# The first transfers of a graph-attention kernel: four of them issued from ScalarE's queue, and one warm-up matmul fewer

## The chip, the cores and the metric

The kernel runs on one core of one Trainium2 chip. A core has TensorE (PE; its weight loads are listed as PEld), VectorE (DVE), ScalarE (ACT), GpSimd (POOL) and SyncE (SP), which here only issues transfers. Sixteen DMA engines move the data. The metric is the device time of one execution in microseconds (us); lower is better.

## The reference

A batch of 16 graphs with 512 nodes of 512 features goes through one layer of graph attention with two directions, 16 heads and, as keys and values, only the first 20 nodes of each graph:

```python
q_exp = jnp.where(row_zero[..., None], 0.0, q[:, None, :])
vcq = jnp.concatenate([exp_v, q_exp], axis=-1)
self_feat = vcq @ W_self.T + b_self
output = self_feat
for d in range(2):
    A = adj_f if d == 0 else jnp.swapaxes(adj_f, 1, 2)
    A = A[:, :, :NONGT, :]
    cond = A.sum(-1)
    vb = A @ w_bias + b_bias
    output = output + _gat_attention(self_feat, cond, vb, Wq[d], bq[d], Wk[d], bk[d], Wout[d], bout[d])
rel = jax.nn.relu(output)
return exp_v + rel
```

In `_gat_attention`, `kv = self_feat[:, :20]`, queries and keys are projections of `self_feat` and `kv`, the weights are a softmax over the 20 keys, masked where `cond` is 0, and the weighted values go through `Wout`. Everything is float32.

## The kernel before, in words

The kernel has a setup and a main loop. The setup (lines 345 to 628) works on the 16 × 20 = 320 key rows of all graphs together. It makes their `self_feat` (called kvn and, with the bias, kvT), the projected keys khT, and from khT and Wq the folded keys g, so that the main loop can take scores straight from `self_feat`. The main loop (lines 641 to 721) goes over the 16 graphs, four node tiles of 128 each: `self_feat` of the tile (line 189), scores (line 249), mask and softmax on VectorE, ScalarE and GpSimd, and, one graph behind, the weighted values (line 314) and the store.

The order is written out by hand (`manual_schedule`): the instructions of each engine run in the order of the code. A transfer belongs to the queue of the engine whose name stands before `dma_start`; `nc.sync` is SP's queue. Eight semaphores serve the transfers issued by SP and ScalarE in turn, so that a transfer waits until the eighth before it has landed.

The change lies in the first 20 us of the setup:

- Line 382: warm-up matmuls of a tile of ones, 128 × 128, into `ps_warm`. A float32 matmul appears in the profile as two rows.
- Lines 385 to 390: `rows` issues one transfer from SP. `kv_rows(k, n)` issues rows k × 128 and on of the key rows' transposed input (`xkv`, 160 KB for one k) and of the feature half of W_self (`ws_v`, 256 KB).
- Lines 392 to 414: the transfers in order. `q_sb` is the condition vector (32 KB), `ws_q` the condition half of W_self (1 MB), `bs_sb` the bias b_self (2 KB), `wk_sb` the key weights (2 × 1 MB), `bk_sb` the key bias (4 KB), `wq_sb` the query weights (2 × 1 MB).
- Lines 417 to 419: GpSimd sums the four chunks of `xkv` into `rsk`, from which PE (line 440) makes the row sums that tell zero rows.
- Lines 428 to 454: PE's order is terms 0 and 1 of the key rows (line 423: four matmuls per term, one for each 128 features of the output), the four matmuls with `ws_q` (line 433), term 2, the row sums (line 440), four small matmuls that turn q (line 445), and term 3. ScalarE copies the product of line 433 out (line 437), its first work; the table load of its activation functions stands before it.
- Lines 455 to 465: per 128 features, a product on GpSimd (the first on VectorE), an addition on VectorE (kvn) and the bias `bs_sb` on ScalarE (kvT).
- Lines 468 to 478: `key_rows`, the projection with `wk_sb` (line 472) and the bias `bk_sb` on ScalarE (line 476). The folded keys (line 550) follow with `wq_sb`.

Of the kernel before, what the change touches and what calls it, by code (L numbers as in the profile page):

```python
# [13 lines left out]
P = 128  # L14
# [4 lines left out]
def gat_kernel(  # L19
# [20 lines left out]
    nc = tc.nc  # L40
# [25 lines left out]
    ws_v = const.tile([P, C, F], F32, name="ws_v")  # L66
# [278 lines left out]
    with tc.tile_pool(name="setup", bufs=1) as sp:  # L345
# [6 lines left out]
        bs_sb = sp.tile([P, C], F32, name="bs_sb")  # L352
        bk_sb = sp.tile([P, 2, C], F32, name="bk_sb")
# [10 lines left out]
        with tc.tile_pool(name="setup_k", bufs=1) as sk:  # L364
            xkv = sk.tile([P, C, BM], F32, name="xkv")
# [13 lines left out]
                    base=-k * DH, channel_multiplier=1,  # L379
                )  # L380
            warm = ps_acc.tile([P, 512], F32, tag="acc", name="ps_warm")
            for _ in range(8):
                nc.tensor.matmul(warm[:, :P], ones, ones, start=True, stop=True)

            def rows(sb, src):
                nc.sync.dma_start(sb, src.rearrange("(c p) f -> p c f", p=P))

            def kv_rows(k, n):
                rows(xkv[:, k : k + n], xkvT[k * P : (k + n) * P])
                rows(ws_v[:, k : k + n], wsT[k * P : (k + n) * P])  # L390

            kv_rows(0, 1)
            kv_rows(1, 1)
            nc.sync.dma_start(q_sb, qT)
            rows(ws_q, wsT[F:])
            kv_rows(2, 1)
            kv_rows(3, 1)
            nc.sync.dma_start(bs_sb, b_self)
            for d in range(2):
                rows(wk_sb[d], wkT[d])  # L400
            nc.sync.dma_start(bk_sb, bk)
            for d in range(2):
                rows(wq_sb[:, d], wq[d])
            nc.sync.dma_start(br_sb, b_row.partition_broadcast(P))
# [92 lines left out]
        with tc.tile_pool(name="setup_g", bufs=4) as sg:  # L497
# [102 lines left out]
            for n, runs in enumerate(bursts):  # L600
# [9 lines left out]
                while done * (len(bursts) - first) < (n + 1 - first) * len(other):  # L610
                    f, args = other[done]
# [23 lines left out]
    with tc.manual_schedule():  # L635
# [102 lines left out]
        for ts, ns, width, banks in parts:  # L738
            for q in range(4):
                c = bass.ds(q // 2 * 2, 2)  # L740
# [65 lines left out]
```

## Time and profile before

| | before |
|---|---|
| median of three runs | 634.22 us (633.94, 636.79, 634.22) |
| the profiled execution | 634.41 us |
| its span | 632.6 us |
| PE busy | 618.7 us, 98% of the span |
| VectorE, GpSimd, ScalarE busy | 508.4, 337.4, 218.1 us |
| moved by DMA | 131.86 MB |
| stretch from 0 to 90 us (setup) | DMA engines nearly full |
| stretch from 90 to 607 us (main loop) | PE busy in all of it |

Times inside the profile count from the start of the span. A group's row gives the line, the engine, the operation, the tile written and the tiles read, the shape, and the number of instructions. PE is busy from the start of a matmul to its modelled end, and matmuls overlap, so the distance between two starts, not the length of one, is the pace. In a timeline row the first number is the start, the second the duration of the merged piece, and the bracket has the idle time before it and what ended it. A row of a stretch has for each engine the busy time and, in brackets, the instructions; then the granted clock, the DMA engines' share and GB/s.

### The profile page before, as it was taken

How to read it: one execution, taken by the hardware profiler on the slowest of the kernel's cores; microseconds unless marked ns; L12 is line 12 of the kernel's file. 1: busy time of each engine (PE TensorE's matmuls, PEld its weight loads, DVE VectorE, ACT ScalarE, POOL GpSimd, SP SyncE). 2: the span in 40 equal slices, each digit the busy share in tenths (PEclk: the TensorE clock that was granted, in tenths of full speed). 3: DMA queues.
4: the chain of work that ended last, by engine and by line, in shares of the span. 5: the costliest groups of instructions: out<-in, count | busy, mean ns of one | idle time of the engine just before them, and what ended most of it. 6: DMA issues, size and time to landing. Idle time of an engine off the chain costs nothing.

```text
span 632.6 us, 16385 instructions
## 1 busy us (share of the span) xinstructions
PE 618.7 (98%) x6814; PEld 383.6 (61%) x6814; DVE 508.4 (80%) x815; ACT 218.1 (34%) x480; POOL 337.4 (53%) x258
## 2 busy tenths in 40 slices
PE   8999999999999999999999999999999999999993
PEld 6655459986565656565655656565656565656542
DVE  0566546879888888888888889797988888888886
ACT  1445321233342424242424233343334242424232
POOL 2405331446556464738392938474655646473853
PEclk9999999999999999999999999999999999999997
DMA  8999998628384565738392909292838465663322
GB/s 287 397 382 321 392 371 249 216 88 268 134 237 165 150 253 127 275 90 313 70 333 42 358 19 339 52 292 107 262 141 248 154 207 196 147 256 102 129 68 101
DMA packets 89569, 131.86 MB, mean 208 GB/s; under 512 B 8888, under 2 KB 59608, under 8 KB 87448
## 3 DMA queue, kind: packets, MB, share of 16 engines
q1 hardware_dynamic: 88824, 129.47, 61.7%
q0 software_dynamic: 672, 1.36, 0.8%
q8 instruction: 53, 0.87, 0.6%
q14 instruction: 20, 0.16, 0.1%
HBM read 90.89 MB, written 39.92 MB: 207 GB/s over the span
## 4 chain that ended last, share of the span: by engine, by line
PE 85%; DVE 2%; ACT 1%; issue 0%; DVEq 0%; ACTq 0%
PE ps_s L249 43%; PE ps_sf L189 33%; PE ps_o L314 6%; PE ps_v L523 1%; ACT o L749 0%; PE ps_nz L172 0%; DVE s L287 0%; DVE mx L278 0%; DVE o L745 0%; DVE s L279 0%; PE ps_g(3, 3, 0, 0, 2)0_778 L550 0%; PE ps_g(3, 2, 0, 1, 2)0_752 L550 0%; PE ps_g(3, 1, 1, 0, 2)0_724 L550 0%; PE ps_g(3, 0, 1, 1, 2)0_701 L550 0%; DVE ps_s L276 0%
## 5 line engine op out<-in xcount | busy, mean ns | idle before, releaser
L249 PE MATMUL ps_s<-g,sf 128*64 128x320 f32 x2048 | 287.6, 433 | 0.0
L249 PEld LDWEIGHTS ps_s<-g,sf 128*64 128x64 f32 x2048 | 155.4, 137 | 116.3 <-issue 6.2
L189 PE MATMUL ps_sf<-x,ws_v 128*64 128x256 f32 (+1 forms) x2048 | 222.0, 371 | 0.0
L189 PEld LDWEIGHTS ps_sf<-x,ws_v 128*64 128x64 f32 x2048 | 151.1, 137 | 67.5 <-issue 1.7
L296 POOL TENSOR_TENSOR s<-s,sm 128x640 f32<-128x640 f32 x63 | 80.1, 1271 | 145.5 <-DVE sm L295 134.8
L269 ACT ACTIVATE s<-s 128x640 f32<-128x640 f32 x63 | 46.5, 738 | 220.9 <-DVE s L264 220.9
L239 POOL TENSOR_TENSOR full<-cq,both 128x640 f32<-128x640 f32 x64 | 99.0, 1547 | 27.6 <-ACT both L230 23.5
L211 POOL TENSOR_TENSOR prod<-prod,wb_sb 128x880 f32<-128x880 f32 x32 | 61.3, 1915 | 56.5 <-ACT prod L210 56.5
L260 DVE TENSOR_TENSOR ps_s<-ps_s,full 128x640 f32<-128x640 f32 x63 | 52.3, 831 | 39.4 <-PE ps_s L249 39.4
L336 POOL TENSOR_TENSOR o<-o,x 128x512 f32<-128x512 f32 x60 | 75.5, 1281 | 0.0
L230 ACT COPY both<-add 64x80 f32<-64x80 f32 x128 | 32.8, 256 | 77.4 <-DVE add L225 76.3
L202 DVE SCALAR_TENSOR_TENSOR sf<-nz,qw,ps_sf 128x236 f32<-128x236 f32 (+1 forms) x128 | 52.6, 458 | 3.5 <-PE ps_sf L189 3.5
L333 ACT ACTIVATE o<-o,bo 128x512 f32<-128x512 f32 x60 | 40.0, 714 | 44.3 <-DVE o L327 44.3
L294 DVE TENSOR_REDUCE sm<-s 128x32 f32<-128x640 f32 x63 | 51.6, 818 | 4.4 <-ACT s L269 0.9
L262 DVE TENSOR_REDUCE mx<-ps_s 128x32 f32<-128x640 f32 x63 | 52.0, 825 | 2.2
L264 DVE TENSOR_TENSOR s<-ps_s,mx 128x640 f32<-128x640 f32 x63 | 51.9, 824 | 2.2
L303 DVE STREAM_TRANSPOSE wt<-s 128x640 f32<-128x640 f32 x63 | 52.5, 834 | 0.0
L314 PE MATMUL ps_o<-wt,vd 32*32 32x256 f32 (+2 forms) x2176 | 46.7, 381 | 4.2 <-issue 2.8
L314 PEld LDWEIGHTS ps_o<-wt,vd 32*32 32x32 f32 x2176 | 31.6, 104 | 19.8 <-issue 12.4
L327 DVE TENSOR_TENSOR o<-ps_o,sf 128x512 f32<-128x512 f32 x60 | 36.3, 668 | 0.0
L152 ACT ACTIVATE xn<-xn 128x512 f32<-128x512 f32 x56 | 34.3, 613 | 0.0
L216 DVE TENSOR_REDUCE cond<-adj 128x80 f32<-128x880 int32 x32 | 33.2, 1036 | 0.2 <-DMA adj<-in_adj 0.2
(205 smaller groups left out, 415.7 us busy)
## 6 DMA issues: line engine op xcount, KB each, us to landing
g<-g_d SPq DMA_DIRECT2D x15, 1280.0 KB, 9.0
g_d<-st SPq DMA_DIRECT2D x16, 1120.0 KB, 6.3
x<-in_xT SPq DMA_DIRECT2D x16, 1024.0 KB, 11.0
out_T<-o SPq DMA_DIRECT2D x61, 256.0 KB, 5.0
xn<-in_xn SPq DMA_DIRECT2D x28, 512.0 KB, 8.7
adj<-in_adj SPq DMA_DIRECT2D x32, 440.0 KB, 7.3
vd<-bd_d SPq DMA_DIRECT2D x64, 128.0 KB, 4.1
nz<-nz_d SPq DMA_DIRECT2D x14, 256.0 KB, 4.7
```

The source lines that it names most:

```text
L189: nc.tensor.matmul(held[0][bass.ts(a, R), i * N // 2 : i * N // 2 + hi - lo], ws_v[:, k, bass.ds((2 * f + i) * P + a * R, R)], xs[b][:, k, ...
L202: nc.vector.scalar_tensor_tensor(sfs[b][:, 2 * f + i, lo:hi], nzs[b][:, lo:hi], qw[:, 2 * f + i, b : b + 1], ps[:, i * N // 2 : i * N // 2 ...
L211: nc.gpsimd.tensor_mul(p, p, wb_sb.unsqueeze(1).to_broadcast([P, 2 * S, L]))
L239: nc.gpsimd.tensor_add(f, cqs[b].unsqueeze(1).to_broadcast(shape), adds[b, nt // 2][:, nt % 2].unsqueeze(2).to_broadcast(shape),)
L249: nc.tensor.matmul(ps[bass.ts(a, R), g, : W // 2], sfs[b][:, k, bass.ds(nt * P + g * R, R)], keys[:, k, a], start=(k == 0), stop=(k == C - 1),
L260: nc.vector.tensor_add(pw, pw, fulls.pop((b, nt)).rearrange("p g h m -> p g (h m)"))
L262: nc.vector.tensor_reduce(mx, p4, AX.X, ALU.max)
L264: nc.vector.tensor_sub(s, p4, mx.unsqueeze(3).to_broadcast(full))
L296: nc.gpsimd.tensor_mul(s, s, sm.unsqueeze(3).to_broadcast(full))
L303: nc.vector.transpose(wts[b][:, nt], s.rearrange("p a h m -> p (a h m)"))
L314: nc.tensor.matmul(banks[q][bass.ts(e, DH)].rearrange("p (t n) -> p t n", n=32), vds[b][r, e, i, q // 2 * 2 + n], wt[r, :, bass.ts(j, 32)] ...
L336: nc.gpsimd.tensor_add(o[:, c], o[:, c], xs[b][:, c])
```

## The change

`rows` takes the queue as an argument, and `kv_rows` takes one chunk k and a queue for its weights. The weights of terms 0 and 1 are issued from ScalarE's queue, and behind them, on the same queue, the biases `bs_sb` and `bk_sb`, which stood on SP's queue after term 3 and after the key weights. SP's queue keeps the `xkv` chunks and all the rest in the old order. The warm-up has seven matmuls instead of eight. Nothing else differs, and what is computed is the same.

```diff
@@ -379,26 +379,27 @@
             warm = ps_acc.tile([P, 512], F32, tag="acc", name="ps_warm")
-            for _ in range(8):
+            for _ in range(7):
                 nc.tensor.matmul(warm[:, :P], ones, ones, start=True, stop=True)
 
-            def rows(sb, src):
-                nc.sync.dma_start(sb, src.rearrange("(c p) f -> p c f", p=P))
-
-            def kv_rows(k, n):
-                rows(xkv[:, k : k + n], xkvT[k * P : (k + n) * P])
-                rows(ws_v[:, k : k + n], wsT[k * P : (k + n) * P])
-
-            kv_rows(0, 1)
-            kv_rows(1, 1)
+            def rows(sb, src, queue=nc.sync):
+                queue.dma_start(sb, src.rearrange("(c p) f -> p c f", p=P))
+
+            def kv_rows(k, queue=nc.sync):
+                rows(xkv[:, k : k + 1], xkvT[bass.ts(k, P)])
+                rows(ws_v[:, k : k + 1], wsT[bass.ts(k, P)], queue)
+
+
+            kv_rows(0, nc.scalar)
+            kv_rows(1, nc.scalar)
+            nc.scalar.dma_start(bs_sb, b_self)
+            nc.scalar.dma_start(bk_sb, bk)
             nc.sync.dma_start(q_sb, qT)
             rows(ws_q, wsT[F:])
-            kv_rows(2, 1)
-            kv_rows(3, 1)
-            nc.sync.dma_start(bs_sb, b_self)
+            kv_rows(2)
+            kv_rows(3)
             for d in range(2):
                 rows(wk_sb[d], wkT[d])
-            nc.sync.dma_start(bk_sb, bk)
             for d in range(2):
                 rows(wq_sb[:, d], wq[d])
```

## The prediction

> **What bounds the kernel now.** I read the busy times and the slices of the page first, then the chain of waits, then the busy times of each engine stretch by stretch, and last the instructions of the first 20 us in order of time, because the change touches nothing later.
>
> ```profile
> span 632.6 us, 16385 instructions
> PE 618.7 (98%) x6814; PEld 383.6 (61%) x6814; DVE 508.4 (80%) x815; ACT 218.1 (34%) x480; POOL 337.4 (53%) x258
> PE 85%; DVE 2%; ACT 1%; issue 0%; DVEq 0%; ACTq 0%
> 10.30:12.00 1.70, 1.08 (x9) 0.16 (x8) 0.00 (x0) 0.00 (x0) 0.62 (x1) 1.00 1.01 307
> 19.70:40.00 20.30, 20.17 (x120) 12.77 (x120) 11.53 (x24) 7.82 (x15) 4.46 (x3) 1.00 1.06 406
> 90.00:607.00 517.00, 517.00 (x5904) 325.19 (x5904) 442.64 (x688) 176.11 (x399) 297.11 (x209) 1.00 0.59 188
> ```
>
> The chain is TensorE, and from 19.7 to 607 us PE is idle for about 0.7 us in all (0.13 from 19.7 to 40, 0.56 from 40 to 90, nothing after). So whatever the start gains or loses goes through to the end one for one, and nothing after 20 us can add to it. The only PE idle time that transfers make is in the stretch from 10.3 to 12.0 us (1.70 − 1.08 = 0.62). Here are the rows around it (start, duration, what, and in brackets the idle time before it and its releaser):
>
> ```profile
> 1.06 3.78 PE L383 MATMUL ps_warm<-ones 128*128 128x128 f32 x16 [1.06 <-DVE ones L369]
> 4.63 5.69 PE L423 MATMUL ps_kv<-xkv,ws_v 128*128 128x320 f32 x16
> 10.95 1.05 PE L433 MATMUL ps_q<-ws_q,q_sb 128*16 128x512 f32 x8 [0.62 <-DMA ws_q<-in_wsT]
> 12.01 1.91 PEld L423 LDWEIGHTS ps_kv<-xkv,ws_v 128*128 128x128 f32 x8 [0.93 <-DMA xkv<-in_xkvT]
> 17.81 0.30 PEld L472 LDWEIGHTS ps_k<-kvT,wk 128*128 128x128 f32 x2 [0.30 <-ACT kvT L465]
> ```
>
> PE warms up, does terms 0 and 1 of the key rows (ps_kv), waits for ws_q, then runs nearly without a break. The semaphore records of the trace give the landing of the last of 16 parts: xkv 0 at 3.06, ws_v 0 at 3.86, xkv 1 at 5.01, ws_v 1 at 6.37, q_sb at 6.54, ws_q at 10.81, xkv 2 at 11.24, ws_v 2 at 11.91, xkv 3 at 12.34, ws_v 3 at 13.02, bs_sb at 13.20, wk 0 at 15.76, wk 1 at 18.41, bk_sb at 18.59. Two of these end a wait of PE: ws_q (row at 10.95) and the pair of term 2 (row at 12.01). The issues, and the DMA engines in half-microseconds from 0 to 20 us:
>
> ```profile
> 1.19 0.42 SPq L386 DMA_DIRECT2D ws_v<-in_wsT  x1
> 2.60 0.43 SPq L394 DMA_DIRECT2D q_sb<-in_qT  x1
> 3.08 0.43 SPq L386 DMA_DIRECT2D ws_q<-in_wsT  x1
> DMA  0003989996779999999999999999999999999999
> GB/s 0 0 0 56 311 247 350 290 232 160 156 221 320 315 319 332 369 383 399 405 355 260 281 375 377 406 393 340 377 397 406 378 356 374 410 391 410 406 410 414
> ```
>
> One issue follows another after about 0.475 us (2.60 to 3.08). The engines are nearly full from 2.0 us on, with a dip from 4.5 to 6.0 us.
>
> **Warm-up.** One matmul fewer is two rows of the sixteen: 3.78 us hold 16 starts of 0.213 us, so the first ps_kv matmul may start 2 × 0.213 = 0.43 us earlier, at 4.20, if ws_v 0 is there (it landed at 3.86; its issue now comes 0.45 us earlier). The first starts of L423 lie 0.533 us apart (5.17, 5.70, 6.24, 6.77 in the rows of PE's weight loads), and from 7.2 us on 0.269: the clock comes up near 7.1 us. If it does so at the same moment, 0.43 us are 0.8 of a slow start, so one fast start fewer is left after it: 0.8 × 0.269 = 0.21 us at the end of terms 0 and 1. By itself that is worth nothing, because PE then waits for ws_q (0.62 + 0.21). Its cover is ws_q; if ws_q came early it would be worth its 0.21.
>
> The rows show the step in start distance once, near 7.1 us. [...]
>
> **The stream.** SP now issues xkv 0, xkv 1, q_sb, ws_q: ws_q is fourth and not sixth, so it goes out 2 × 0.475 = 0.95 us earlier (2.13). ScalarE issues ws_v 0 at about 0.74, ws_v 1, bs_sb and bk_sb. The bytes ahead of the end of ws_q are the same, plus two tiny transfers. Their price is in the landings: bs_sb came 0.18 us after ws_v 3, bk_sb 0.18 us after wk 1, both directly behind them in the queue, so 0.36 us for both. Best end: all the earlier issue counts, −0.95 + 0.36 = −0.59; without the tiny ones' price −0.95. Worst end: the engines were full anyway and the start gains nothing, +0.36. Between: the start of the stream. ws_v 0's issue moves from 1.19 to 0.74, and in the slices from 1.5 to 2.5 us only xkv 0 was there to be moved; that is worth up to 0.45, so −0.45 + 0.36 = −0.09. The dip of 4.5 to 6.0 us (156 to 221 GB/s against 290 to 350 before it) says that the bytes alone aren't the limit there, so I take the middle of −0.59 and −0.09, −0.35 us for ws_q. Term 2's pair stands behind ws_q on the same queue and comes with it: also −0.35.
>
> [...]
>
> **What the edit moves past, at no cost.** Eight semaphores serve the transfers in turn, and each new transfer waits for the landing of the eighth before it. In the built order of the changed kernel xkv 2 waits for ws_v 0, ws_v 2 for xkv 0, xkv 3 for xkv 1, ws_v 3 for ws_v 1 (landings 3.06 to 6.37; before: issues at 3.55, 4.10, 4.58, 5.27). They are queued behind ws_q's 1 MB, over 2.5 us of stream at 400 GB/s, so an issue 0.5 us later stays hidden. wk 1 now waits for ws_q's landing (it was issued at 8.34, now near 10.5); it is hidden behind wk 0, which was in the stream until 15.76, and is needed only when the second group of L472 starts near 20 (landed 18.41). If wk 0 were drained first, the wait of wk 1 would cost its 1.6 us of slack and then PE. wq waits for bs_sb and bk_sb, long landed. On ScalarE four issues (1.9 us) precede the table load:
>
> ```profile
> 1.68 1.28 ACT L437 ACT_TABLE_LOAD   x1 [1.68 <-DVE ps_q L371]
> 12.06 0.58 ACT L437 COPY q<-ps_q 128x512 f32<-128x512 f32 x1 [9.10 <-PE ps_q L433]
> ```
>
> The load ends near 3.9 instead of 2.96, and the first work is at 12.06: 8 us of cover. bs_sb (needed at 17.19) and bk_sb (20.53) were not waited for.
>
> **Where the gain goes.** After 12 us PE runs without a break up to the row at 15.59; then GpSimd's three products behind L445 and the kvT rows set L472 (four waits, 1.3 us in all). All of it hangs on L433 and term 2, so it shifts whole. The term 3 sums wait for xkv 3 (12.34, on GpSimd 12.47 to 13.33, used at 14.00): 0.67 us of slack, more than the shift. Cap: PE can gain its idle 0.62, the 0.06 before term 2, and the 0.21, together 0.89 us.
>
> **Sum.** The profiled execution took 634.41 us, 1.8 of it around the span of 632.6; the median is 634.22, 0.19 lower. 634.22 − 0.35 = 633.87, so **633.9 us**; its own range is the cap to the stream's −0.09: 633.3 to 634.1.
>
> **Rivals.**
> - *The bytes decide.* ws_q lands no earlier, at worst 0.36 us later: 634.2 to 634.6. For it: the engines' 9s, and three of ws_q's sixteen parts landing at 10.5 to 10.8 where the middle one landed at 8.7, which no queue changes. Against: the dip.
> - *The slow parts vanish.* If ws_q's last parts come with its middle one, PE takes the whole cap: 634.22 − 0.89 = 633.3. [...] Against: nothing shows what made them slow.
> - *The clock stays low (slower).* Place: the seam between warm-up and first ps_kv matmul. If ws_v 0 lands after about 4.2 us, PE idles there; if the slow pace then lasts through all 16 rows of terms 0 and 1, the some 11 starts that were fast cost 11 × (0.533 − 0.269) = 2.9 us, less the 0.62 wait that hides a part: +2.3, 636.5. For it: the cover was 4.43 − 3.86 = 0.57 us, and the edit uses 0.43 of it. Against: ws_v 0 is issued 0.45 us earlier.
> - *The edit doesn't take effect.* ScalarE issues late. Its queue is free at 0.67 and the built order puts the four issues before its first wait, so unlikely: PE's first row would wait for ws_v 0, about 634.7.
>
> **Numbers.** Chances: forecast 0.48, bytes decide 0.27, slow parts vanish 0.10, clock stays low 0.12, no effect 0.03. The known runs are 633.94, 634.22 and 636.79, so a median can move by itself. The range runs from 632.7 (the cap below the lowest run, 633.05, less the 0.3 between the two lowest) to 636.0 (three quarters of the clock's price, +1.7); outside it are most of the clock case and odd medians. Half a per cent is 3.2 us, about what a measurement of this kernel can tell from no change; no gain here reaches it (cap 0.89) and the clock's 2.3 doesn't either, so: faster 0.02, within 0.94, slower 0.04.
>
> **What would show it.** In the changed profile: 14 ps_warm rows, the first L423 start near 4.2, ws_q issued at 2.13, the wait before L433 and L433's start at 10.6 (forecast), 10.95 or later (bytes), 10.1 (slow parts gone); L472 near 17.5. The forecast is wrong if the start distance of L423 stays at 0.53 past 7.1 us, or if L472's start moves and the span doesn't follow.

## The result and the profile after

| | before | changed |
|---|---|---|
| median of 22 runs each | 635.39 us (633.94 to 638.21) | 633.84 us (632.48 to 636.50) |
| ratio | | 0.9973, 95% interval 0.9961 to 0.9985 |
| runs above 636 us | 10 of 22 | 2 of 22 |
| the profiled execution, and its span | 634.41, 632.6 us | 633.99, 632.2 us |

The ratio is 1.7 us less (1.0 to 2.5). It lies within the half per cent that the prediction took for the limit of such a measurement, and clear of no change. The two profiled executions differ by 0.4 us only, and the medians by 1.55: with 22 runs in place of three the kernel before has a median 1.2 us higher than the one the prediction started from. What the profiles show and what the runs show are therefore two questions. Of the two runs of the changed kernel above 636 us, 2.7 and 2.8 us lie outside the span, where most runs have 1.8 us; both spans are 633.7 us.

First the profiles. These are the span and the busy times of the changed kernel (busy time, share of the span, instructions):

```profile
span 632.2 us, 16380 instructions
PE 617.2 (98%) x6812; PEld 368.5 (58%) x6812; DVE 507.6 (80%) x815; ACT 217.9 (34%) x480; POOL 337.9 (53%) x258
```

And PE's first rows in its timeline (start and length in us, engine, line, operation; in brackets the idle time just before and what ended it; line numbers are one higher from the change on):

```profile
1.06 3.36 PE L383 MATMUL ps_warm<-ones 128*128 128x128 f32 x14 [1.06 <-DVE ones L369]
4.39 5.46 PE L424 MATMUL ps_kv<-xkv,ws_v 128*128 128x320 f32 x16
10.69 1.05 PE L434 MATMUL ps_q<-ws_q,q_sb 128*16 128x512 f32 x8 [0.83 <-DMA ws_q<-in_wsT]
11.78 1.91 PEld L424 LDWEIGHTS ps_kv<-xkv,ws_v 128*128 128x128 f32 x8 [0.96 <-DMA xkv<-in_xkvT]
17.58 0.30 PEld L473 LDWEIGHTS ps_k<-kvT,wk 128*128 128x128 f32 x2 [0.30 <-ACT kvT L466]
```

The ps_q row starts at 10.69 (10.95 before), term 2 at 11.78 (12.01), the key projection at 17.58 (17.81): 0.23 to 0.26 us earlier, and the wait for ws_q is still there and longer, 0.83 us. The first ps_kv matmul starts at 4.39, not 4.20: ws_v 0 landed at 4.35, later than before (3.86).

The issues on both queues in the same kernel's timeline, with ScalarE's table load and copy:

```profile
0.74 0.90 ACTq L386 DMA_DIRECT2D ws_v<-in_wsT  x2
0.74 0.86 SPq L386 DMA_DIRECT2D xkv<-in_xkvT  x2
1.66 0.45 ACTq L395 DMA_DIRECT2D bs_sb<-in_b_self  x1
2.12 0.43 SPq L386 DMA_DIRECT2D ws_q<-in_wsT  x1
2.69 1.28 ACT L438 ACT_TABLE_LOAD   x1 [2.69 <-DVE bqbd L372]
11.80 0.59 ACT L438 COPY q<-ps_q 128x512 f32<-128x512 f32 x1 [7.83 <-PE ps_q L434]
```

And its view of the DMA engines from 0 to 20 us, in half-microseconds (busy share in tenths, and GB/s):

```profile
DMA  0007379999788899999999999989999999999999
GB/s 0 0 0 51 30 269 406 401 400 237 182 193 198 306 387 368 404 387 395 400 409 404 398 413 401 340 328 377 373 397 393 389 401 410 397 406 414 414 406 401
```

ws_q is issued at 2.12 (3.08 before). The stream starts slower (30 and 269 GB/s from 2.0 to 3.0 us; before 311 and 247), then runs at 400 GB/s from 3.0 to 4.5 us, where it ran at 350, 290 and 232; the dip near 5 us stays. ws_q's last part landed at 10.55 (10.81 before).

### The profile page after: what moved, and what is told of

The parts are those of the page before. It is cut to its first block, busy times and chain, and to the rows that moved or that the text cites. A ratio compares the mean times of both kernels' runs of the same rounds, so it can differ in the third digit from the quotient of the medians.

```text
span 632.2 us, 16380 instructions
## 1 busy us (share of the span) xinstructions
PE 617.2 (98%) x6812; PEld 368.5 (58%) x6812; DVE 507.6 (80%) x815; ACT 217.9 (34%) x480; POOL 337.9 (53%) x258
## 4 chain that ended last, share of the span: by engine, by line
PE 85%; DVE 2%; ACT 1%; issue 0%; DVEq 0%; ACTq 0%
PE ps_s L249 43%; PE ps_sf L189 33%; PE ps_o L314 6%; PE ps_v L524 1%; ACT o L750 0%; PE ps_nz L172 0%; DVE s L287 0%; DVE mx L278 0%; DVE o L746 0%; DVE s L279 0%; PE ps_g(3, 2, 0, 1, 2)0_751 L551 0%; PE ps_g(3, 0, 1, 1, 2)0_700 L551 0%; PE ps_g(3, 1, 1, 0, 2)0_723 L551 0%; PE ps_g(3, 3, 0, 0, 2)0_777 L551 0%; DVE ps_s L276 0%
## 5 line engine op out<-in xcount | busy, mean ns | idle before, releaser
L249 PEld LDWEIGHTS ps_s<-g,sf 128*64 128x64 f32 x2048 | 145.8, 137 | 125.4 <-issue 6.2
L189 PEld LDWEIGHTS ps_sf<-x,ws_v 128*64 128x64 f32 x2048 | 146.7, 137 | 71.9 <-issue 1.7
```

The costliest lines, as they stand in the source:

```text
L189: nc.tensor.matmul(held[0][bass.ts(a, R), i * N // 2 : i * N // 2 + hi - lo], ws_v[:, k, bass.ds((2 * f + i) * P + a * R, R)], xs[b][:, k, ...
L249: nc.tensor.matmul(ps[bass.ts(a, R), g, : W // 2], sfs[b][:, k, bass.ds(nt * P + g * R, R)], keys[:, k, a], start=(k == 0), stop=(k == C - 1),
```

## The experiments

"Before" in each comparison is the kernel before, run on the same chip in the same rounds. Landing times are from the semaphore records of the profiled execution.

**One part at a time.** Warm-up alone:

```diff
-            for _ in range(8):
+            for _ in range(7):
                 nc.tensor.matmul(warm[:, :P], ones, ones, start=True, stop=True)
```

> The kernel before with seven warm-up matmuls instead of eight, nothing else. Theory A (the gain of 1.7 us in the medians comes from the transfers): the wait for ws_q (0.62 us) swallows what PE gains, so the time is that of the kernel before within 0.4 us, the first L423 start is 4.2 and L433 still starts when ws_q lands. Theory B (it comes from the warm-up): at least 1.0 us faster than the kernel before.

Measured: 635.81 us, before 635.97; ratio 0.9989 (0.9968 to 1.0009). The warm-up alone brings nothing that these rounds can tell. But its profile, taken of an execution of 637.78 us with a span of 634.8 us, holds a key to the spread. (3.0 us of this execution lie outside the span, against 1.8 us in the profile of before; only the some 2 us by which the span is longer are to be explained by its rows.) PE's rows in the timeline, and then the stretches of 3.41 us that follow the clock's records (behind the stretch and its length the busy time of PE, PEld, VectorE, ScalarE and GpSimd, with the number of instructions; the third number from the end is the granted clock):

```profile
4.21 4.97 PE L423 MATMUL ps_kv<-xkv,ws_v 128*128 128x320 f32 x16
11.24 1.23 PE L433 MATMUL ps_q<-ws_q,q_sb 128*16 128x512 f32 x8 [2.06 <-DMA ws_q<-in_wsT]
12.40 3.88 PE L423 MATMUL ps_kv<-xkv,ws_v 128*128 128x320 f32 x8
```

```profile
5.16:8.57 3.41, 3.41 (x14) 2.38 (x13) 0.00 (x0) 0.00 (x0) 0.59 (x1) 1.00 0.89 279
8.57:11.98 3.41, 1.35 (x11) 0.26 (x9) 0.00 (x0) 0.00 (x0) 0.31 (x1) 1.00 1.03 362
11.98:15.39 3.41, 3.41 (x10) 2.02 (x7) 0.00 (x0) 0.58 (x1) 1.41 (x2) 0.50 1.04 387
15.39:18.80 3.41, 3.41 (x19) 2.70 (x18) 1.49 (x4) 0.00 (x0) 0.84 (x1) 1.00 1.05 389
```

There is a chain in these rows. Here the clock came up at 5.15 us, not at 7.1, so PE was done with terms 0 and 1 at 9.18 and waited 2.06 us for a ws_q that landed at 11.10. In the stretch from 8.57 to 11.98 PE was busy for 1.35 us only; in the next the granted clock is 0.50. Term 2 took 3.88 us instead of 2.39, the ps_q matmuls 1.23 instead of 1.05: 1.67 us lost. In this execution the PE that was early lost more than the one of before that was late.

The lowered stretch is 3.41 us long, here and in e8 further down, and in the fourteen executions profiled in this study the clock came up anywhere from 4.08 to 7.10 us.

The queue part alone (eight warm-up matmuls, the rest as in the change):

> The changed kernel with the old eight warm-up matmuls: the queue part alone. Theory A: the whole gain, 1.0 to 2.2 us faster than the kernel before. Theory B: within 0.6 us of it.

Measured: 634.29, before 635.97; ratio 0.9966 (0.9948 to 0.9985). As far as these rounds can tell, the whole gain is in the queues.

The weights alone:

```diff
-            nc.scalar.dma_start(bs_sb, b_self)
-            nc.scalar.dma_start(bk_sb, bk)
...
             kv_rows(3)
+            nc.sync.dma_start(bs_sb, b_self)
             for d in range(2):
                 rows(wk_sb[d], wkT[d])
+            nc.sync.dma_start(bk_sb, bk)
```

> Only the two weight transfers go from ScalarE's queue; both biases stay where they were, eight warm-up matmuls. Theory A1 (the earlier start of the stream and of ws_q counts): 1.0 to 2.2 us faster than before, ws_q landed by 10.3 since no small transfer stands ahead of it. Theory A2 (the biases on SP's queue cost it, by their turn in the eight semaphores): within 0.5 us of before.

Measured: 634.27, before 635.97; ratio 0.9968 (0.9947 to 0.9988). ws_q landed at 9.94. So the weights carry the gain. Its row for the ps_q matmuls, against 10.69 in the changed kernel, with the biases ahead:

```profile
10.07 1.05 PE L434 MATMUL ps_q<-ws_q,q_sb 128*16 128x512 f32 x8 [0.92 <-DMA ws_q<-in_wsT]
```

The biases alone, the mirror image:

```diff
             kv_rows(1, 1)
+            nc.scalar.dma_start(bs_sb, b_self)
+            nc.scalar.dma_start(bk_sb, bk)
             nc.sync.dma_start(q_sb, qT)
...
-            nc.sync.dma_start(bs_sb, b_self)
...
-            nc.sync.dma_start(bk_sb, bk)
```

> Only the two biases go from ScalarE's queue, ahead of q_sb; the weights stay on SP, eight warm-up matmuls. Theory A1: no gain, 0 to 0.5 us slower than before, because two small transfers (0.18 us each) stand ahead of ws_q. Theory A2: 1.0 us or more faster than before.

Measured: 635.75, before 635.97; ratio 0.9996 (0.9971 to 1.0021); ws_q landed at 11.02. Nothing gained. The profiled execution took 636.24 us with the clock at full speed in the first 20 us; it lost its time elsewhere, at the first weighted values in the main loop (line 314; the kernel before does these 128 rows from 137.46 on in one piece of 2.76 us; the view here ends at 141 us):

```profile
137.47 0.63 PE L314 MATMUL ps_o<-wt,vd 32*32 32x256 f32 x6
139.36 2.00 PE L314 MATMUL ps_o<-wt,vd 32*32 32x256 f32 x91 [1.26 <-issue]
```

The values vd themselves had landed by 123.93. What came late is the adjacency `adj`. The code writes `ps_o` into the same pool of four tiles (`ps_acc`) that `ps_sf` uses, so PE needs VectorE to have read `ps_sf` (line 202), and VectorE had first waited for `adj` (line 216). Its rows in the kernel before, and then here:

```profile
126.93 1.07 DVE L216 TENSOR_REDUCE cond<-adj 128x80 f32<-128x880 int32 x1 [0.18 <-DMA adj<-in_adj]
```

```profile
128.68 1.07 DVE L216 TENSOR_REDUCE cond<-adj 128x80 f32<-128x880 int32 x1 [1.93 <-DMA adj<-in_adj]
138.40 0.86 DVE L202 SCALAR_TENSOR_TENSOR sf<-nz,qw,ps_sf 128x256 f32<-128x256 f32 x2
```

VectorE ends line 202 at 139.26, and PE goes on at 139.36. `adj` was issued at 122.21 (120.37 in the profile of before), since SP's queue had waited ahead of it for a write (`bd_d`) that landed at 119.86 (118.01). The profiles of the runs further down agree: PE's 128 rows take 1.83 us longer here, 0.88 in e8, 0.64 in e11, 0.32 in e5 and 0.22 in e7, where VectorE waited for this `adj` for 1.93, 0.98, 0.73, 0.42 and 0.28 us. In the nine other profiles it waited 0.24 us at most, and the rows take 2.75 or 2.76 us. So there is a second place where a transfer comes just in time or not.

**Is it the clock or the landing?** Theory C says that in part of the runs the wait for ws_q lets the clock fall; theory S that only the landing counts. Four matmuls of ones are put into the wait, which shortens PE's idle time and moves no transfer; their result isn't used:

```diff
             for k in range(2):
                 for fc in range(C):
                     kv_terms(fc, k)
+            for _ in range(4):
+                nc.tensor.matmul(ps_q[:, 1, 384:512], ones, ones, start=True, stop=True)
```

> The kernel before with four more matmuls of ones put between terms 0 and 1 and the ws_q matmuls, so that PE is busy for 0.85 us more of its wait (8 rows of some 0.107 us). Their result is not used. Theory C (in part of the runs of the kernel before the wait for ws_q lets the clock fall for 3.4 us, which costs 1.9 us): the wait is 1.2 us at most, the clock doesn't fall, the median is 0.7 to 1.5 us under the kernel before's and the runs above 637 are gone. Theory S (only the earlier landing counts): no gain, 0 to 0.3 us slower.

Measured: 634.83 (633.13 to 635.77), before 636.00 on that chip; ratio 0.9986 (0.9971 to 1.0001). The interval just touches 1, but of twelve runs none is above 636, of the thirty of before fifteen are. The profiled execution is a telling one, since its clock came up at 4.08 us, the earliest of all. PE's rows in the timeline:

```profile
4.37 4.58 PE L423 MATMUL ps_kv<-xkv,ws_v 128*128 128x320 f32 x16
8.79 1.05 PE L432 MATMUL ps_q<-ones 128*128 128x128 f32 x8
11.35 1.05 PE L435 MATMUL ps_q<-ws_q,q_sb 128*16 128x512 f32 x8 [1.51 <-DMA ws_q<-in_wsT]
```

And the two stretches that follow the clock's records (busy time of PE first, the granted clock third from the end):

```profile
7.50:10.91 3.41, 2.35 (x14) 1.76 (x12) 0.00 (x0) 0.00 (x0) 0.00 (x0) 1.00 1.02 344
10.91:14.32 3.41, 2.93 (x15) 1.59 (x16) 0.00 (x0) 0.59 (x1) 1.72 (x2) 1.00 1.03 380
```

ws_q landed at 11.22, as late as in e1 (11.10). Without the fill PE would have been idle from about 8.8 on, and the first stretch busy for some 1.3 us by these rows, as in e1. With it the stretch is busy for 2.35 us, and the clock stays at 1.00.

The same fill in the changed kernel:

> The changed kernel with the same four matmuls in its wait. Theory C: its wait hardly ever lets the clock fall, so the fill gains 0 to 0.4 us on the changed kernel (633.8), and the difference to e5 is the landing alone, 0.2 to 0.7 us. Theory S: equal to the changed kernel or 0.2 us slower, and the difference to e5 is the full 1.7.

Measured: 634.46, before 636.00; ratio 0.9983 (0.9969 to 0.9997). The two kernels with the fill differ by 0.37 us in the medians, as C had it; S wanted 1.7. And the fill doesn't help the changed kernel: C's 0 to 0.4 of gain was a miss, the ratio is if anything nearer to 1 than without it.

The fill with the weights alone:

> Weights alone on ScalarE's queue (biases left on SP behind term 3 and the key weights), eight warm-up matmuls, and the four matmuls in the wait: the candidate that may beat both. Both theories: ws_q lands near 10.0, since no small transfer is ahead; with C some 0.3 us under e6, 633.3 or less; with S the same as e3, 634.3.

Measured: 634.51, before 636.00; ratio 0.9980 (0.9964 to 0.9996); ws_q landed at 10.02. A miss: no better than e6. In its profile the clock came up at 7.01, so the fill ended at 11.2, after ws_q, and PE waited for nothing but its own work.

The wait made longer, in the kernel before:

```diff
             nc.sync.dma_start(q_sb, qT)
-            rows(ws_q, wsT[F:])
             kv_rows(2, 1)
+            rows(ws_q, wsT[F:])
             kv_rows(3, 1)
```

> The kernel before with ws_q issued after the pair of term 2 and not ahead of it: 416 KB more in front of it, about 1.0 us at 400 GB/s. Theory C: PE waits 1.6 us or more in nearly every run, the clock falls in most of them, and the median is 2 to 3.5 us above the kernel before. Theory S: the wait alone, 0.5 to 1.0 us slower, since term 2 no longer waits.

Measured: 639.16 (637.58 to 641.05), before 636.00; ratio 1.0064 (1.0041 to 1.0087). All five runs lie above the median of before by 1.5 us or more. S allowed 1.0; C's 2 to 3.5 holds the 3.2 between the medians (the ratio gives 4.1, 2.6 to 5.5). The profile has the fall again, first in PE's rows of the timeline:

```profile
12.08 1.27 PE L433 MATMUL ps_q<-ws_q,q_sb 128*16 128x512 f32 x8 [2.32 <-DMA ws_q<-in_wsT]
13.28 3.84 PE L423 MATMUL ps_kv<-xkv,ws_v 128*128 128x320 f32 x8
```

and then in the two stretches:

```profile
9.37:12.78 3.41, 1.09 (x10) 0.16 (x8) 0.00 (x0) 0.00 (x0) 0.26 (x1) 1.00 1.06 396
12.78:16.19 3.41, 3.41 (x10) 1.93 (x7) 0.00 (x0) 0.58 (x1) 0.60 (x1) 0.50 1.05 391
```

It also lost 0.9 us at the rows of line 314, behind VectorE's wait for `adj`, so not all of the 3.2 us need be the clock's.

**A version without the wait.** Three pairs ahead of ws_q, and term 2 ahead of the ps_q matmuls:

```diff
             kv_rows(1, nc.scalar)
+            kv_rows(2, nc.scalar)
             nc.sync.dma_start(q_sb, qT)
             rows(ws_q, wsT[F:])
-            kv_rows(2)
             kv_rows(3)
...
-            for k in range(2):
+            for k in range(3):
                 for fc in range(C):
                     kv_terms(fc, k)
...
-            for fc in range(C):
-                kv_terms(fc, 2)
```

> A version meant to beat both: the weights of terms 0, 1 and 2 on ScalarE's queue, all three pairs issued ahead of q_sb and ws_q, and PE does term 2 before the ws_q matmuls; biases stay on SP, eight warm-up matmuls. ws_q has 416 KB more ahead of it and lands near 11.0, but PE has 2.15 us more of work before it needs it (until 11.3 to 12.2), so there is no wait for it and no window in which the clock can fall. What is new is a wait of about 0.65 us for ScalarE's copy behind the ws_q matmuls. Theory C: the row-sum matmul starts near 13.2 (changed kernel: 13.77), no run above 636, median 633.0 to 633.7. Theory S (only the landing of ws_q counts): 0.5 to 1.0 us slower than the weights alone (634.3).

Measured: 634.19 (632.94 to 635.60), before 635.82; ratio 0.9968 (0.9953 to 0.9983): as good as the change, not better. The wait for ws_q is gone, and PE's own start takes its place:

```profile
4.63 7.62 PE L424 MATMUL ps_kv<-xkv,ws_v 128*128 128x320 f32 x24
12.19 1.05 PE L434 MATMUL ps_q<-ws_q,q_sb 128*16 128x512 f32 x8
14.04 0.78 PE L439 MATMUL ps_q<-rsk,ones 128*128 128x320 f32 x2 [0.80 <-ACT q L438]
```

The clock came up at 6.64, PE was ready at 12.19, and the copy behind it cost 0.80 us; the row sums start at 14.04, 0.8 later than expected. ws_q had landed at 9.70 and not near 11.0, although 416 KB more stood ahead of it.

**The kernel before again**, against itself and in two single executions, without an edit:

> The kernel before once more, against itself: the ratio should be 1 within its interval. Theory C: in four of ten of its runs the clock falls during the wait for ws_q, so that the times spread over 634 to 638 and the profile, if it is one of the slower executions (636 or more), shows the granted clock at one half for 3.4 us near 12 us and a wait of 1.5 us or more; a profile under 635 shows neither. Theory S: the spread comes from elsewhere, and a profile of 636 or more shows the clock at full speed in the first 20 us.

> The kernel before, one more profiled execution, to catch one of its slower executions. [...] Theory S: at 636 or more, term 2 takes 2.4 us and the loss lies elsewhere, as in e4, where it was a wait for vd at 137 us.

> As e11, a second execution: with four or five in ten over 636, one of the two should be one.

Measured: e10 635.08, ratio 0.9999 (0.9979 to 1.0019), five of twelve runs above 636. The three profiled executions took 634.85, 635.77 and 634.23 us. None is above 636, none has the clock down in the first 20 us (it came up at 6.21, 6.31 and 5.55; PE waited 1.35, 1.51 and 1.33 us), and in all three term 2 takes 2.39 us. ws_q landed at 11.10, 11.31 and 10.76. Of e11's 1.4 us more of span than in the first profile, 0.6 come at the rows of line 314, behind `adj`. So no profile caught the fall of the clock in the kernel before itself; it was caught with one warm-up matmul fewer and with ws_q late.

The runs that weren't profiled have something to say too, because the mean granted clock over the span is on record for each. A fall of 3.41 us takes 3.41 / 2 / 634 = 0.0027 off it. In the 94 runs of the change, e2, e3, e5, e6, e7 and e9 it is 0.994, 0.993, 0.992, 0.990 or 0.988 and nothing else (the profiles have 7.5 to 14.8 us at half clock at the end of the kernel, which gives these values). In the 103 runs of the kernel before from e1 on it is 0.991, 0.989, 0.987, 0.986 or 0.985 in 20, values that lie about one fall below the others, and all 20 took over 636 us. So falls do occur in the kernel before. But of its 47 runs over 636 us, eight have 0.994 or 0.993, which leaves no room for a fall, since no run of any kernel has more than 0.994: there the time went elsewhere, as in e4's profile (636.24 us, 0.994). The other 19 can be either. The mean doesn't tell where in the kernel a fall lies.

## Why the prediction was right, and where it wasn't

**The way and the place: right.** As far as rows account for it, the gain comes with ws_q's earlier landing, through PE's wait for it, and it goes through to the end: the shift of 0.23 us at the key projection is 0.23 us at 95 us too, grows to 0.37 at 100 us, and the span is 0.4 shorter. The warm-up is worth nothing by itself (e1). The table load behind four issues, the late wk 1 and the biases on ScalarE cost nothing that a row shows.

**The price of the stream: its parts.** "Between: the start of the stream … worth up to 0.45" failed: two queues at once didn't bring the first pair earlier, ws_v 0 landed at 4.35 and not before 3.86. The two small transfers were taken at 0.36 us; with them ahead ws_q landed at 10.55, 10.52 and 10.32 (the change, e2, e6), without at 9.94 and 10.02 (e3, e7), so about 0.5. The times don't show it (634.29 in e2, 634.27 in e3, with intervals over 2 us wide), and in e4, where the biases had landed by 4.09, ws_q came at 11.02, as without them. What gained was the issue of ws_q. The sum was −0.35 for ws_q; the two profiles have −0.26, but the profile of before was one of its better executions. Over the seven with the weights on SP's queue and ws_q in its old place (before, e1, e4, e5, e10, e11, e12) ws_q landed at 10.76 to 11.31, in the mean at 11.05. Against 10.46 for the three with the change's transfers that is −0.59.

**The step that failed: the cap.** "PE can gain its idle 0.62, the 0.06 before term 2, and the 0.21, together 0.89 us" was read from one execution and held for that one alone. The measured gain is 1.7 us (1.0 to 2.5). The idle 0.62 belongs to a clock that came up at 7.1 us; with an earlier clock PE waits longer (1.33 us in e12, with the clock up at 5.55 and ws_q landed at 10.76), and in e1 and e8 the clock then fell and term 2 paid 1.5 us. "Nothing after 20 us can add to it" failed for the same reason: the first profile has no wait there, e4's lost 1.83 us behind `adj`. The prediction had the clock as a rival, but at the wrong seam (warm-up to first matmul) and with the wrong sign: it feared that the change would lower the clock, and the change takes falls away.

How much that is can be estimated. PE finishes terms 0 and 1 about 0.5 us earlier for each us that the clock comes up earlier (done at 10.33 with the clock up at 7.10 in before, at 9.56 with 5.55 in e12). With a landing at 11.05 and the start 0.1 later the idle time is 11.15 − 10.33 = 0.82 us, plus half of what the clock is earlier than 7.1. The clock fell at 2.06 and 2.32 us of idle time in a stretch and held at 1.56 and less; where between them the limit lies no run shows. If it is near 1.75, a clock up before 5.25 lets it fall. In the fourteen profiles the clock came up between 4.08 and 7.10; if that range is taken as evenly filled, which is assumed, this would be some (5.25 − 4.08) / 3.02 = 39% of the runs. With a landing 0.59 earlier the bound is 4.1, the lower end of the range, so next to none. 39% fewer falls at 1.67 us are 0.65 us, with the 0.59 of the landing 1.2, which lies in the interval. The record of the clock puts the falls lower, at some 20 to 39 of 103 runs of before (19 to 38%, by how many of the 19 are counted) and none that can be told in the 82 of the change, e2, e3, e6, e7 and e9, which gives 0.3 to 0.6 us and with the landing 0.9 to 1.2: the lower end of the measured 1.0 to 2.5. The counts go the same way: above 636 us are 10 of 22, 16 of 35, 15 of 30 and 11 of 23 runs of before, and 2 of 22 of the change and 0 of 12 in each of e2, e3, e6, e7 and e9. The fill, which touches no transfer, has 0 of 12 in the kernel before.

**What stays open.** How the 1.7 us divide. The landing and the falls leave up to about 0.8 us of it without a row. The waits for `adj` are a candidate: VectorE's wait cost PE 0.3 to 1.8 us in four of the eight profiles with the weights on SP's queue (e4, e5, e8, e11), and 0.2 us in one of the six with them on ScalarE's (e7). Whether the change takes part in that wasn't tried. Nor does any run tell in which share of before's runs above 636 us the clock fell at the wait for ws_q; e1 and e8 show it there, and the fill acts there.

**The number.** 633.9 was forecast and 633.84 measured, but partly by chance: the forecast took 0.35 from a median of three that was 1.2 us low. The rivals: "the bytes decide" fell with e2 and e3; "the slow parts vanish" didn't happen (ws_q's middle part landed at 8.96, its last at 10.55); "no effect" fell with the rows; "the clock stays low" didn't happen, although its condition did (ws_v 0 landed at 4.35, after 4.2): the clock came up at 6.22 in the changed kernel's profile.

## What to carry to other kernels

A wait of PE can have two prices, its length and what runs slowly after it (2.06 us and 1.67 us in e1); look at several executions before you set a cap from one, above all where the times of equal runs spread by more than the effect. Making the engine earlier ahead of a fixed wait (e1) brought nothing; making the transfer earlier did (e2, e3), and filling the wait took the runs above 636 us away, though its gain in the median is not clear of noise (e5). Move what the wait is for. And where a wait is put down to "issue", look at who last used the tile that is written: the row's own inputs had long landed.

## What the runs showed of the hardware that I had not expected

- The mean granted clock of an unprofiled run can tell that the clock fell: 20 of 103 runs of before have a value about one fall of 0.0027 below those of the 94 runs of the change, e2, e3, e5, e6, e7 and e9.
- The granted clock fell to 0.50 behind a stretch of 3.41 us in which PE had been busy for 1.35 us (e1), 1.09 in e8; behind stretches with 1.85 (e2: wait of 1.55 us), 1.90 (e11), 2.35 (e5) and 2.50 us (the change) it stayed at 1.00.
- ws_q's sixteen parts landed over 2.0 to 3.2 us in thirteen profiles (8.18 to 10.81 in before), but over 0.8 us in e9 (8.93 to 9.70), with three pairs of 416 KB ahead of it. Why some parts are late in the one and not in the other isn't known.
- Two queues that started together delivered the first pair later (4.35) than one queue that issued it in turn (3.86). In the other profiles it is 4.29 to 4.54 against 3.81 to 4.03. Why isn't known.
